# A two-layer convolution kernel: the first image's row differences on GpSimd, and the next image's group-mean product handed to TensorE two steps later

## The chip, the cores and the metric

The kernel runs on one core of a Trainium2 chip. The metric is the time on the device, in microseconds (us), from start to end of one launch; a launch does the whole batch of eight images and both layers. Time before: 1755.58 us, the median of three runs (1754.55 to 1759.55). The profile below is of one execution, whose span from first to last instruction is 1756.5 us.

## The reference, cut to what matters

All data are fp32. The input `x` has 8 images of 128 channels by 64 x 64 pixels. Two layers are each added to their input:

```python
x = x + L0(_gn(x))   # deformable 3x3 convolution, batch norm, relu
x = x + L1(_gn(x))   # mixture of 3x3 convolutions
```

`_gn` normalises each group of four channels over an image by its mean and variance. The change lies in the second layer:

```python
pooled = jnp.mean(x, axis=(2, 3))
scores = jax.nn.sigmoid(pooled @ gate_w.T + gate_b)
_, indices = jax.lax.top_k(scores + gate_bias, 2)       # two of four experts
weights = scores at indices, divided by their sum        # w_dense: (8, 4), zero elsewhere
ye  = conv2d(x, w_e) + b_e for each of the four experts
out = sum_e(ye * w_dense[e]) + conv2d(x, shared_w) + shared_b
```

A convolution is linear in its weights, so for one image the chosen experts and the shared kernel can be mixed into a single 3 x 3 kernel before anything is convolved. That is what the kernel does.

## The kernel before, in words

**Stages.** `dense()` is the first layer and takes the first 1372 us. `layer1()` is the second; it fills the rest. (A second pass through both follows only if the offsets of the deformable convolution leave a fixed reach; for this input it is skipped.)

**The second layer's arithmetic.** The 3 x 3 convolution is done two output rows at a time, with a Winograd-like transform in the vertical direction. From the normalised, padded image `pad2` each group `g` of 16 output rows (NG = 4 groups per image) gets three row differences and sums in a tile `v`, made by `transform(g, which, engine)`:

- `which` 1: odd rows plus even rows, 128 partitions x 528 elements (L1018)
- `which` 2: even rows minus odd rows, 528 elements (L1020)
- `which` 0: rows minus the rows two below, 1056 elements (L1022); it serves both outer products

The mixed weights are transformed in the same way into four sets: `wmix[:, 0]`, `u1`, `u2`, `wmix[:, 2]`. Each of the four products `j` of a group (order 1, 2, 0, 3) is then three matrix products, one for each horizontal tap `kx`, 128 x 128 weights by 512 columns. In the profile each such fp32 product is two TensorE instructions, so a product `j` is 6 instructions, a group 24, an image 96, eight images 768. `collect` empties the four PSUM results of a group: `j` = 1 on ScalarE (L1080, into `t`), the others on VectorE (L1084, L1088, L1090), and the output rows go out by DMA.

**The order is written by hand.** The stage is under a manual schedule: each engine gets its instructions in the order in which the Python code emits them, and takes them in that order. Image `b`'s products are emitted by the last loop of `layer1()`. Everything that image `b + 1` needs ahead of its products is a generator, `prepare(b + 1)`, whose `yield`s cut it in steps. After each product `j` the loop takes two steps of it (three after `j` = 3), so 36 in an image; they are counted from 1 here. Before the change the steps are:

- steps 1 to 10: for eight chunks of 512 pixels, batch norm and relu of the first layer's result on ScalarE (L928), the residual addition on GpSimd (L930; for image 0 every second one is on VectorE), and two steps later the chunk's statistics on VectorE (L932)
- step 11: the statistics put together into `mv` on VectorE (L937)
- step 12: the product `pm` on TensorE that averages the means over a channel group (L940)
- step 13: the deviation `d` and `e` on VectorE; step 14: the product `pv` of the variances on TensorE (L950); steps 15 and 16: scale and shift (one GpSimd instruction at L111 among them)
- steps 17 to 20: the gate product `pg` (L972), scores, the choice of experts; the normalisation into `pad2` (L963, ScalarE) is strewn over these and the next steps
- steps 21 to 25: mixing of the weights on VectorE (L1039: four instructions, L1047, and L1050 to L1052 for `u2` and `u1`)
- steps 26 to 33: the twelve transforms; step 34: the results are handed over

**Image 0 has no image ahead of it to hide behind.** `prepare(0)` runs to its end before any product. It is cut more finely: the weights are mixed for one `kx` at a time (so L1039 takes 384 elements and not 1152, and L1050 to L1052 take 128), and the products of its first group go `kx` by `kx`, all four `j` in each, so that TensorE can begin when the weights of `kx` = 0 are there. In the kernel before, transforms (0, 1) and (0, 2) of image 0 are on GpSimd, (0, 0) is on VectorE after the weights of `kx` = 0 (L1054), and the nine of groups 1 to 3 are on VectorE after all the weights (L1056 to L1062). The additions of image 1 come next in GpSimd's order, its statistics next in VectorE's.

Image 1's chunks 0 and 1 are emitted after group 0's product `j` = 1, its chunks 2 and 3 after the collection of that product on ScalarE. So ScalarE reaches chunk 2 only when TensorE has finished `j` = 1 of group 0.

Of the kernel before, what the change touches and what calls it, by code (L numbers as in the profile page):

```python
# [57 lines left out]
def deform_moe_conv(  # L58
# [18 lines left out]
    nc = tc.nc  # L77
# [777 lines left out]
    def layer1():  # L855
# [6 lines left out]
        with ExitStack() as st:  # L862
# [4 lines left out]
            NG = 4  # L867
# [52 lines left out]
            def prepare(b, made):  # L920
# [14 lines left out]
                    yield  # L935
                mv = small.tile([P, 2], F32, name="mv")
                nc.vector.bn_aggr(mv, stats)  # L937
                yield
                pm = ps_s.tile([P, 4], F32, name="pm", tag="pss")
                nc.tensor.matmul(pm[:, 0:1], lhsT=gsel, rhs=mv[:, 0:1], start=True, stop=True)  # L940
                yield
# [20 lines left out]
                def normalise(c):  # L962
                    nc.scalar.activation(  # L963
                        pad2[:, 1 + 8 * c : 9 + 8 * c, 1 : W + 1],
                        x1[:, c * CH : (c + 1) * CH].rearrange("p (h w) -> p h w", w=W),
                        AF.Identity, bias=shift, scale=scale,
                    )
# [45 lines left out]
                def transform(g, which, engine):  # L1013
                    v, r = vs[g], 2 * TR * g
                    even = pad2[:, r + 2 : r + 2 * TR + 2 : 2]
                    odd = pad2[:, r + 1 : r + 2 * TR + 1 : 2]
                    if which == 1:
                        engine.tensor_tensor(v[:, 2 * TR : 3 * TR], odd, even, ALU.add)  # L1018
                    elif which == 2:
                        engine.tensor_tensor(v[:, 3 * TR :], even, odd, ALU.subtract)  # L1020
                    else:
                        engine.tensor_tensor(  # L1022
                            v[:, 0 : 2 * TR], pad2[:, r : r + 2 * TR],
                            pad2[:, r + 2 : r + 2 * TR + 2], ALU.subtract,
                        )
# [4 lines left out]
                if b == 0:  # L1030
                    for c in range(4, NCH):
                        normalise(c)
                    transform(0, 1, nc.gpsimd)
                    transform(0, 2, nc.gpsimd)

                for kx in range(3) if b == 0 else (slice(0, 3),):
                    part = wmix[:, :, kx]
                    for e in range(NE):
                        nc.vector.scalar_tensor_tensor(  # L1039
                            part, experts[:, e, :, kx], wd[:, e : e + 1],  # L1040
                            part if e else shared[:, :, kx], ALU.mult, ALU.add,
                        )
                        if b:
                            normalise(4 + e)
                            yield
                    if b or kx == 1:
                        nc.vector.scalar_tensor_tensor(  # L1047
                            wmix[:, 1, 1], ident, inv, wmix[:, 1, 1], ALU.mult, ALU.add
                        )
                    nc.vector.tensor_tensor(u2[:, kx], part[:, 0], part[:, 2], ALU.add)  # L1050
                    nc.vector.tensor_tensor(u1[:, kx], u2[:, kx], part[:, 1], ALU.add)  # L1051
                    nc.vector.tensor_tensor(u2[:, kx], u2[:, kx], part[:, 1], ALU.subtract)  # L1052
                    if kx == 0:
                        transform(0, 0, nc.vector)  # L1054
                    yield
                for g in range(NG):  # L1056
                    if b or g:
                        transform(g, 1, nc.vector)
                        transform(g, 2, nc.vector)
                        yield  # L1060
                        transform(g, 0, nc.vector)
                        yield  # L1062
                made[b] = vs, (wmix[:, 0], u1, u2, wmix[:, 2]), bmix

            made, todo = {}, []
            for _ in prepare(0, made):
                pass
            for b in range(B):
                load(b + 2)
                ahead_of = prepare(b + 1, made) if b + 1 < B else iter(())  # L1070
                vs, us, bmix = made.pop(b)
                for g in range(NG):
# [115 lines left out]
```

## Time and profile before

| what | value |
|---|---|
| time, median of three | 1755.58 us |
| TensorE busy over the span | 1643.6 us (94%) |
| VectorE busy | 1189.7 us (68%) |
| ScalarE busy | 944.4 us (54%) |
| GpSimd busy | 939.6 us (53%) |
| last instruction of the first layer's batch statistics (L636) | 1372.8 us |
| first product of the second layer (L1102) | 1397.61 us |
| last of the 36 product instructions ahead of image 1's `pm` starts, ends | about 1414.6, 1415.16 us |
| image 1's `pm` starts on TensorE | 1426.38 us |
| first product after image 1's `pv` | 1432.20 us |
| first product of image 1 | about 1455.8 us |

How to read it: the busy share is an average over two very different stages. The rows with a point in time (microseconds from the start of the span, taken from the timeline in order of time) are those for the change: they all lie in the 60 us in which the second layer starts. From image 1 on, an image takes 42.0 us (from 1455.8 to 1497.8 TensorE is busy for all of it).

### The profile page before, as it was taken

What the parts mean: (1) busy time and instruction counts of PE and PEld (TensorE: products, weight loads), DVE (VectorE), ACT (ScalarE), POOL (GpSimd) and SP (SyncE); (2) the same over time, 40 slices, a digit from 0 to 9 for tenths busy, and PEclk for the clock granted to TensorE, in tenths of its full rate; (3) what the DMA queues carried; (4) which work ended last, traced back from release to release, by engine and by line L of the source; (5) the groups of instructions that cost most, each with busy time, mean ns of one, the idle gap of its engine ahead of it and who ended that gap; (6) DMA issues with size and microseconds to landing.
All of it is one profiled execution on the core that took longest, in us unless ns stands there. A gap on an engine that the chain in (4) does not pass through costs nothing. (4 is left out here: it accounts for less than half of the span.)

```text
span 1756.5 us, 21264 instructions
## 1 busy us (share of the span) xinstructions
PE 1643.6 (94%) x6490; PEld 931.0 (53%) x6490; DVE 1189.7 (68%) x1910; ACT 944.4 (54%) x1970; POOL 939.6 (53%) x1516
## 2 busy tenths in 40 slices
PE   4399999999999999999999999999999479999998
PEld 2155565566566556655665666566666234444443
DVE  4464874687467648755874587477665688888882
ACT  1465765576476557655765676476665323333330
POOL 3375576558557746764675657557763322322210
PEclk9599999999999999999999999999999689999999
DMA  4643774585368438744863675376663603444311
GB/s 133 124 121 93 154 179 106 115 194 137 93 133 203 121 82 168 180 106 103 193 150 94 134 187 143 98 137 151 161 158 87 267 25 144 155 156 154 123 49 62
DMA packets 197598, 235.84 MB, mean 134 GB/s; under 512 B 133964, under 2 KB 148048, under 8 KB 197478
## 3 DMA queue, kind: packets, MB, share of 16 engines
q0 software_dynamic: 94976, 124.94, 32.4%
q1 hardware_dynamic: 100556, 109.04, 20.7%
q8 instruction: 57, 0.93, 0.2%
q10 hardware_dynamic: 1946, 0.41, 0.1%
q14 instruction: 63, 0.52, 0.1%
HBM read 183.00 MB, written 50.82 MB: 133 GB/s over the span
## 5 line engine op out<-in xcount | busy, mean ns | idle before, releaser
L495 DVE TENSOR_TENSOR s<-xwts,ywts 100x324 f32<-100x324 f32 x968 | 691.5, 759 | 186.4 <-PE pq L506 160.1
L506 PE MATMUL pq<-s,xt 100*128 100x324 f32 x1936 | 696.8, 441 | 12.4 <-DVE s L495 6.7
L512 ACT COPY samples<-pq 128x324 f32<-128x324 f32 x968 | 423.9, 443 | 463.8 <-PE pq L506 458.1
L521 PE MATMUL py<-samples,dw_sb 128*128 128x384 f32 (+1 forms) x1584 | 625.1, 476 | 2.2 <-ACT y L532 2.1
L441 POOL DMA_DIRECT2D xwts<-tabx x863 | 527.2, 621 | 96.9 <-DMA ywts<-taby 52.6
L425 POOL DMA_DIRECT2D ywts<-taby x528 | 302.4, 587 | 365.8 <-DVE s L495 309.4
L506 PEld LDWEIGHTS pq<-s,xt 100*128 100x128 f32 x1936 | 322.4, 190 | 185.9 <-issue 48.7
L521 PEld LDWEIGHTS py<-samples,dw_sb 128*128 128x128 f32 x1584 | 299.5, 189 | 138.5 <-ACT y L532 6.5
L478 PE MATMUL pt<-ident,picked 128*100 128x128 f32 x968 | 194.2, 275 | 41.8 <-ACT picked L465 33.7
L478 PEld LDWEIGHTS pt<-ident,picked 128*100 128x100 f32 x968 | 121.6, 128 | 181.7 <-issue 80.0
L535 DVE BATCH_NORM_STATS2 ystats<-y 128x6 f32<-128x384 f32 (+1 forms) x88 | 48.2, 547 | 218.5 <-ACT y L532 218.5
L1102 PE MATMUL pc<-v,u 128*128 128x512 f32 x384 | 172.8, 599 | 9.2 <-DVE u L1051 9.2
L1102 PE MATMUL pc<-v,wmix 128*128 128x512 f32 x384 | 176.4, 605 | 0.0
L485 ACT COPY xt<-pt 100x512 f32<-100x512 f32 (+1 forms) x264 | 147.5, 559 | 2.2 <-PE pt L478 2.2
L313 PE MATMUL pc<-pad,offw_sb 128*32 128x504 f32 (+1 forms) x1152 | 142.2, 601 | 1.9 <-ACT pad L278 1.9
L1102 PEld LDWEIGHTS pc<-v,u 128*128 128x128 f32 x384 | 72.4, 190 | 98.3 <-issue 85.1
L1080 ACT ACTIVATE t<-pc,bmix 128x512 f32<-128x512 f32 x32 | 22.0, 687 | 182.5 <-issue 94.3
L1102 PEld LDWEIGHTS pc<-v,wmix 128*128 128x128 f32 x384 | 72.3, 191 | 88.6 <-issue 84.9
L457 ACT COPY picked<-pad 128x900 f32<-128x900 f32 x88 | 91.7, 1042 | 9.0 <-DMA xwts<-tabx 9.0
L608 ACT COPY samples<-samples 128x1188 f32<-128x1188 f32 x80 | 95.9, 1198 | 0.0
L930 POOL TENSOR_TENSOR x<-x,xt 128x512 f32<-128x512 f32 x32 | 47.0, 1496 | 85.3 <-ACT x L928 85.3
L930 POOL TENSOR_TENSOR pad<-pad,pad 128x512 f32<-128x512 f32 x28 | 39.6, 1442 | 71.6 <-ACT pad L928 71.5
(137 smaller groups left out, 897.1 us busy)
## 6 DMA issues: line engine op xcount, KB each, us to landing
ywts<-taby POOLq DMA_DIRECT2D x528, 116.0 KB, 4.3
pad<-in_x_dram SPq DMA_DIRECT2D x48, 512.0 KB
xwts<-tabx POOLq DMA_DIRECT2D x173, 116.0 KB, 3.8
out_dram<-yo SPq DMA_DIRECT2D x32, 512.0 KB
xwts<-tabx POOLq DMA_DIRECT2D x172, 92.8 KB, 3.8
yd<-y SPq DMA_DIRECT2D x80, 192.0 KB
xwts<-tabx POOLq DMA_DIRECT2D x173, 69.6 KB, 3.6
pad<-yd SPq DMA_DIRECT2D x16, 512.0 KB
```

The costliest lines, as they stand in the source:

```text
L313: nc.tensor.matmul(pc[32 * j : 32 * j + 32].rearrange("p (h w) -> p h w", w=W)[:, :, lo:hi], lhsT=offw_sb[:, k, :], rhs=pad[:, r : r + 8, ...
L425: engine.dma_start(out=y_wts[g % 2][r * Q : (r + NR) * Q, r].rearrange("p b c -> p (b c)"), in_=bass.AP(tensor=y_table[b].tensor, offset=y ...
L441: engine.dma_start(out=x_wts[g % 3][q:QQ:Q, :, lo:hi].rearrange("p t a b c -> p t (a b c)"), in_=bass.AP(tensor=x_table[b].tensor, offset= ...
L457: nc.scalar.copy(picked[g % 2][:, 1 : NT1 - 1], bass.AP(tensor=one.tensor, offset=one.offset, ap=[list(one.ap[0]), [T, NT1 - 2], [W, Q], [ ...
L478: nc.tensor.transpose(pt[0:QQ, c], picked[g % 2][:, c0 + c].rearrange("p y x -> p (y x)"), ident,)
L485: nc.scalar.copy(xts[g][0:QQ, c0 : c0 + n], pt[0:QQ, 0:n])
L495: nc.vector.tensor_tensor(s[0:QQ], x_wts[g % 3][0:QQ, c].rearrange("p a k r -> p k r a"), y_wts[g % 2][0:QQ, :, :, T * c : T * c + T].rear ...
L506: nc.tensor.matmul(pq.rearrange("p k r a -> p (k r a)"), lhsT=xts[g][0:QQ, c], rhs=ss.pop(n)[0:QQ].rearrange("p k r a -> p (k r a)"), star ...
L512: nc.scalar.copy(samples[g % 2][:, :, 2 : T + 2, T * c : T * c + T], pq)
L521: nc.tensor.matmul(py[:, first:], lhsT=dw_sb[:, 3 * ky + kx], rhs=samples[g % 2][:, n, first + ky : T + ky, kx : kx + W], start=(i == 0), ...
L608: nc.scalar.copy(samples[g % 2][:, :, 0:2], samples[(g - 1) % 2][:, :, T : T + 2])
L1102: nc.tensor.matmul(pc, lhsT=us[j][:, kx], rhs=vs[g][:, rows, kx : kx + W], start=(kx == 0), stop=(kx == 2),)
```

## The change

It has two parts. First, all twelve transforms of image 0 are given to GpSimd, in the order 1, 2, 0 of each group, and are emitted ahead of the mixing of its weights; VectorE makes none of them any more. For the later images they stay where they were. Second, for image 1 alone, two empty steps are put between the statistics `mv` and the product `pm`: `pm` and everything after it in `prepare(1)` come two steps later, so that `pm` stands on TensorE behind product `j` = 0 of group 1, and no longer ahead of it. The aim is to free VectorE at the start of the layer and to give TensorE work to do while image 1's statistics are not there.

```diff
                 mv = small.tile([P, 2], F32, name="mv")
                 nc.vector.bn_aggr(mv, stats)
-                yield
+
+                for _ in range(3 if b == 1 else 1):
+                    yield
                 pm = ps_s.tile([P, 4], F32, name="pm", tag="pss")
                 nc.tensor.matmul(pm[:, 0:1], lhsT=gsel, rhs=mv[:, 0:1], start=True, stop=True)
...
                 if b == 0:
                     for c in range(4, NCH):
                         normalise(c)
-                    transform(0, 1, nc.gpsimd)
-                    transform(0, 2, nc.gpsimd)
+                    for g in range(NG):
+                        for which in (1, 2, 0):
+                            transform(g, which, nc.gpsimd)
...
                     nc.vector.tensor_tensor(u2[:, kx], u2[:, kx], part[:, 1], ALU.subtract)
-                    if kx == 0:
-                        transform(0, 0, nc.vector)
                     yield
-                for g in range(NG):
-                    if b or g:
-                        transform(g, 1, nc.vector)
-                        transform(g, 2, nc.vector)
-                        yield
-                        transform(g, 0, nc.vector)
-                        yield
+                for g in range(NG if b else 0):
+                    transform(g, 1, nc.vector)
+                    transform(g, 2, nc.vector)
+                    yield
+                    transform(g, 0, nc.vector)
+                    yield
                 made[b] = vs, (wmix[:, 0], u1, u2, wmix[:, 2]), bmix
```

## The prediction, made before the changed kernel was run

> **What bounds the kernel now.** I read the page's forty slices first (43.9 us each).
>
> ```profile
> PE   4399999999999999999999999999999479999998
> PEclk9599999999999999999999999999999689999999
> ```
>
> TensorE is full except in the first two slices and in slices 32 and 33 (1361 to 1449 us) and at the very end, where the granted clock sinks too. The change touches nothing earlier, and after it an image takes 42.0 us of unbroken TensorE work. So only those holes are at stake. The waits from 1310 us on name them:
>
> ```profile
> PE pm L940 <- DVE mv L937: 25.4, 2, 14.2
> PE pc L1102 <- DVE u L1051: 9.2, 1, 9.2
> ```
>
> (who waited for whom: total us, times, longest). Image 0's `pm` took 14.2 us, so image 1's took 25.4 - 14.2 = 11.2. The chain of waits shows what lay ahead of it (start us, us, what):
>
> ```profile
> 1409.22 1.70 DVE v L1020
> 1410.92 2.25 DVE v L1022
> 1413.17 1.69 DVE v L1018
> 1414.86 1.69 DVE v L1020
> 1416.55 2.23 DVE v L1022
> 1418.78 1.20 DVE stats L932 x2
> ...
> 1425.96 0.38 DVE mv L937
> 1426.38 0.59 PE pm L940 x2
> 1426.97 5.25 PE pc L1102 x6
> ```
>
> The reader is to see VectorE doing image 0's transforms until 1418.8, then image 1's statistics, then `mv`, with TensorE waiting from 1415.16 to 1426.38. The six product instructions after it take 5.25 us; six others later take 2.70 (a step of 0.43 warm, 0.86 cold), so the hole costs 11.2 + 2.6 = 13.8 us. The timeline shows what VectorE and GpSimd do to each other:
>
> ```profile
> 1389.65 1.10 POOL L1018 TENSOR_TENSOR v<-pad 128x528 f32<-128x528 f32 x1 [2.31 <-ACT pad L963]
> 1389.95 0.82 DVE L997 SCALAR_TENSOR_TENSOR wd<-rank,score 128x4 f32<-128x4 f32 x1
> ...
> 1394.52 2.84 POOL L930 TENSOR_TENSOR x<-x,xt 128x512 f32<-128x512 f32 x2 [2.71 <-ACT x L928]
> 1395.00 1.23 DVE L1050 TENSOR_TENSOR u<-wmix 128x128 f32<-128x128 f32 x1
> 1396.27 1.23 DVE L1051 TENSOR_TENSOR u<-u,wmix 128x128 f32<-128x128 f32 x1
> 1397.54 0.29 DVE L1052 TENSOR_TENSOR u<-u,wmix 128x128 f32<-128x128 f32 x1
> ```
>
> L997, four elements, takes 0.82 us beside a GpSimd transform, against 0.16 for a later image: it ends when the transform ends. L1050 and L1051 take 1.23 beside GpSimd's additions, against 0.29 for L1052 after them. In the chain above, each VectorE transform beside additions takes 1.07 us more than alone (1.69 against 0.62, 2.25 against 1.17). They take turns, one for one.
>
> [...]statistics and the PSUM collections beside additions keep their 0.67 us.[...] The trace: full clock until about 1418.4, 3.2 us after the last product, half until 1432.
>
> **The change part by part.**
>
> *Nine transforms leave VectorE at the end, and (0, 0) in the middle.* From 1406.11 to 1418.78 is 12.7 us off the chain to `mv`, and 1.17 off the chain to the second weights.
>
> *GpSimd gets ten more.* A 528-element transform steps at 1.06 to 1.10 (1389.65, 1390.71)[...]. The 1056-element one isn't in the trace on GpSimd. Low: twice 1.06 = 2.12[...]. I take 2.17. All twelve alone: 4 x (1.08 + 1.08 + 2.17) = 17.3 us, 1389.65 to 1407. ScalarE's normalisation (done 1393.7) stays ahead of them.
>
> *The price is taken from VectorE's weight mixing,* which now meets transforms all along. By turns, a VectorE share[...] (0.62 at 528, 1.17 at 1056): 0.47 for L1039 at 384, 0.20 for L1050 to L1052 at 128, 0.07 for tiny ones. The walk: GpSimd's (0,0) from 1391.80 to 1393.97, L1005 1394.04; (1,1) 1395.12, L1008 1395.2; then nine turns: (1,2) + first L1039 1396.75; (1,0) + L1039 1399.39; (2,1) + L1039 1400.94; (2,2) + L1039 1402.49; (2,0) + L1050 1404.86; (3,1) + L1051 1406.14; (3,2) + L1052 1407.42; (3,0) + L1039 for `kx` 1 1410.06. Two additions with L1039s end at 1413.14, then GpSimd waits for ScalarE. VectorE goes on alone at its steps of before (0.65, 0.26, 0.33): `u1` of `kx` 1 at 1414.8, of `kx` 2, another 3.5 us on, at 1418.3.
>
> *TensorE's start* follows L1051, now 1406.3 and not 1397.6, 8.7 us later. First `kx`, cold: 5.3, to 1411.6. It waits 3.3 for `u1`, from 1414.9 does eight instructions (3.44), from 1418.4 eight more, to 1421.84. Then eighteen, one `j` more than before, 18 x 0.43 = 7.74: 1429.6. Before, the same place was 1432.06 (`pv`, with `pm` inside).
>
> *When `mv` is there.* ScalarE's chunk 2 is queued behind the collection of `j` = 1, which waits for 1418.4 + 0.86. Collection 1419.5, chunk 2 1420.1, first addition 1421.0 (0.88 after, as at 1408.10 to 1408.98). Six additions, nothing contending: 7.91 (the six of the next image, from 1460.07): 1428.9. Last statistics and `mv` 1.15: 1430.05. So `pm` at about 1430.1 waits 0.5 us, and products go on at 1430.25, against 1432.20. `pv`, still ahead in the new order, costs 0.14. Sum: **-1.8 us**. A cold restart at 1414.9 adds 1.7 to 3.4[...]: 0 to +1.5. I weigh it one in four.
>
> *The two steps* move `pv` behind `j` = 3 and `pg` into group 2. Behind `pm` on TensorE are image 0's products, each 2.6 us ahead of the next of these, time enough for `d`, `e` (0.6) and the scale (1.2). The later end of image 1's preparation: `pg` at 1435.6 against 1434.9, mixing done near 1448.5, transform (0,1) and (0,2) 1450.3 after one more collection; image 1 starts at about 1454. Margin 3.5 us, so nothing. PSUM has seven buffers and the collections come earlier than before: nothing. Loads and output DMA hang on points that hardly move: nothing.
>
> So the gain of a 13.8 us hole is nearly all spent on a start 8.7 us later and the 3.3 us hole in the first group. From 1755.58, weighing -1.8 and the cold case: 1754.1.
>
> **The rivals.**
>
> *L1039 doesn't contend* (only L1050 to L1052 and the small ones do). For it: no L1039 row is seen slowed. Against: L997 is the same kind. Then four L1039s run to 1397.2, L1051 ends 1399.85, later ones 1405.9 and 1411.5; TensorE does its last `kx` from 1411.6 to 1415.0, eighteen more to 1422.8; `mv` 10.6 after 1412.7, at 1423.3. Products at 1423.5 against 1432.2, less 0.14: -8.5, **1747.1**. With no contention at all `pm` would be at 1418.9 and the gain 13; the rows above exclude it.
>
> *VectorE doesn't get in between transforms,* since they stand ready one behind another, so that mixing waits for all of GpSimd's work. For it: one row only (L997) shows it getting in there; against: the chain's strict turns. From 1393.97, nine transforms 13.0 and two additions 2.15: 1409.2. Then L1005 to L1008, four L1039 and two: TensorE at 1413.1, and with `kx` after `kx` 5.3 + 3.4 + 3.4 + 7.7: 1433; `mv` 10.6 after 1422.9, `pm` 1433.6. +1.7, with a longer cold start +3: **1758**, slower.
>
> **How the numbers follow.** Forecast 0.60, faster rival 0.22, slower rival 0.18. Two in three of the faster rival's cases are at or above 1747. The slower one ends past 1760 if[...] the clock goes cold twice (+3), or image 1's 3.5 us margin is used up. Range 1747 to 1760. The bound of 0.3% is 5.3 us: faster takes the faster rival and a little of the forecast, 0.25; slower half of its rival and a little, 0.13; same 0.62.
>
> **What would show it.** L1039 for image 0 near 1.5 to 2.6 us instead of 0.62, and L1050 to L1052 above 1.2: turns are right; L1039 still at 0.62: the faster rival. The first product near 1406; a second wait of about 3 us on `u`; `pm` with under 1 us of wait near 1430; L1022 on GpSimd at 2.2 alone, about 2.6 with a turn. Wrong if image 1's first product waits for `v` or `u`, or if `mv` comes more than 2 us after TensorE asks.

## The result and the profile after

| | time, median | against before in the same comparison |
|---|---|---|
| before | 1757.57 us | |
| after | 1765.26 us | ratio 1.0044, 95% interval 1.0026 to 1.0063 |
| after, a second comparison | 1762.16 us (before there: 1756.99) | ratio 1.0037, 1.0026 to 1.0048 |

The change makes the kernel slower by about 0.4%: 7.7 us in the first comparison, 5.2 in the second. The forecast was 1754.1 us in a range of 1747 to 1760; the measured time lies above it.

The slices of the profile after, of the same kind as those shown of before (TensorE's busy tenths and its granted clock; a slice is 44.1 us):

```profile
PE   4399999999999999999999999999999299999998
PEclk9599999999999999999999999999999699999999
```

The second hole is narrower (one poor slice, a 2, where there were a 4 and a 7), and yet the kernel is slower. TensorE's waits from 1360 us on say where the rest is (who waited for whom: total us, times, longest):

```profile
PE pc L1102 <- DMA pad<-in_x_dram: 17.4, 1, 17.4
PE pm L942 <- DVE mv L937: 17.3, 2, 14.2
PE pc L1102 <- DVE u L1054: 3.2, 1, 3.2
```

The 17.4 is the wait for the first product (it is put down to a DMA; in the second execution the same wait is put down to `u` at L1054). It was 9.2. The `pm` row still has two waits: image 0's 14.2, as before, and another of 17.3 - 14.2 = 3.1. The timeline shows that this one is no longer image 1's:

```profile
1410.33 3.43 PE L1102 MATMUL pc<-v,u 128*128 128x512 f32 x4 [17.42 <-DMA pad<-in_x_dram]
...
1418.73 2.43 PE L1102 MATMUL pc<-v,u 128*128 128x512 f32 x4 [3.25 <-DVE u L1054]
...
1432.57 2.76 PE L1102 MATMUL pc<-v,wmix 128*128 128x512 f32 x6
1435.16 0.36 PE L942 MATMUL pm<-mv,gsel 128*128 128x1 f32 x2
...
1459.20 5.31 PE L1102 MATMUL pc<-v,u 128*128 128x512 f32 x12
...
1469.54 5.31 PE L1102 MATMUL pc<-v,u 128*128 128x512 f32 x12
1478.00 0.47 PE L942 MATMUL pm<-mv,gsel 128*128 128x1 f32 x2 [3.15 <-DVE mv L937]
1478.34 4.43 PE L1102 MATMUL pc<-v,wmix 128*128 128x512 f32 x6
```

The reader is to see: the first product, the wait of 3.25 us for the second tap's weights, image 1's `pm` at 1435.16 right behind its six new predecessors, without a wait; image 1's first product at 1459.20; and then image 2's `pm` at 1478.00, which waits 3.15 us where before it waited for nothing, and whose six followers take 4.43 us, not 2.84, on a clock that has fallen (granted 0.50 from 1478.16 to 1481.57, 1.00 around it). In the profile of before the same place reads:

```profile
1471.27 0.28 PE L940 MATMUL pm<-mv,gsel 128*128 128x1 f32 x2
1471.41 2.84 PE L1102 MATMUL pc<-v,wmix 128*128 128x512 f32 x6
```

**The scale.** The first layer, untouched by the change, ends at different times from execution to execution (GpSimd's L872, an instruction at the start of the second layer, stood at 1373.89 in the profile of before and at 1378.45 in that of after). So all below is counted from the start of L872, and the second layer is cut in two: its start, from L872 to image 1's first product, and the rest, from there to the end.

| execution | start | rest | second layer |
|---|---|---|---|
| before, profile | 81.9 | 300.7 | 382.6 |
| before, three further executions | 79.9, 79.9, 77.1 | 300.7 each | 380.6, 380.6, 377.8 |
| after, profile | 80.8 | 305.8 | 386.5 |
| after, two further executions | 79.1, 80.8 | 305.8 each | 384.9, 386.6 |

Means: start 79.7 before and 80.2 after, rest 300.7 and 305.8. Together +5.6 us, inside the interval of the second comparison (0.26 to 0.48% of 1757 us: 4.6 to 8.4). The start gives nothing; the rest loses 5.1 us.

### The profile page after: what moved, and what is told of

It is laid out like the page before. It is cut to its first block, busy times and chain, and to the rows that moved or that the text cites. A ratio compares the mean times of both kernels' runs of the same rounds, so it can differ in the third digit from the quotient of the medians.

```text
span 1765.0 us, 21267 instructions
## 1 busy us (share of the span) xinstructions
PE 1644.1 (93%) x6490; PEld 930.9 (53%) x6490; DVE 1192.1 (68%) x1900; ACT 944.9 (54%) x1970; POOL 954.6 (54%) x1526
## 5 line engine op out<-in xcount | busy, mean ns | idle before, releaser
L1102 PE MATMUL pc<-v,u 128*128 128x512 f32 x384 | 173.2, 600 | 20.7 <-DMA pad<-in_x_dram 17.4
L930 POOL TENSOR_TENSOR x<-x,xt 128x512 f32<-128x512 f32 x32 | 43.7, 1397 | 80.8 <-ACT x L928 80.8
```

Of the source, the lines that this page charges most:

```text
L1102: nc.tensor.matmul(pc, lhsT=us[j][:, kx], rhs=vs[g][:, rows, kx : kx + W], start=(kx == 0), stop=(kx == 2),)
```

## The experiments

Theory A: VectorE and GpSimd take turns (one instruction of the one, then one of the other), so that the moved transforms delay the mixing about as much as they free later; and the loss is image 2's statistics. Rivals: the first layer is slower for good by how the program lies (B) or merely spreads (C); the empty steps help and something else loses.

**The changed kernel again.**

> The changed kernel, once more, to see how much of its 7.7 us lies in the first layer, whose instructions are the same. In the two profiles at hand the second layer took 382.6 us before (1373.9, where GpSimd takes up L872, to 1756.5) and about 386.5 us after; the first layer took 4.5 us longer in the profile of after. Theory A (the loss is in the second layer: image 2's statistics come 3.15 us after TensorE asks for them, with a cold clock behind it): second layer again 386 to 387 us, the first layer anywhere within the 5 us by which executions of before differ; time 3 to 5 us above before. Rival B (the first layer is slowed for good, by where the program lies): first layer again 4 us longer than in before, time 7 to 8 us above before.

Measured: ratio 1.0037; second layer 384.9 us, 1.1 under the expected span: the first tap's products ran on the half clock for longer (their eight instructions took 3.75 and 3.17 us and not 3.43 and 1.89), so the wait for the second tap was 1.68 us and not 3.25, and the second tap's first four instructions took 1.98 us and not 2.43. First layer end 1374.30: only 0.4 us above the profile of before. Image 2's wait: 3.15 again. B loses its main evidence.

**The empty steps for image 2 too.**

```diff
-                for _ in range(3 if b == 1 else 1):
+                for _ in range(3 if b in (1, 2) else 1):
```

> After, with the two empty steps for image 2 as well, so that TensorE does six more product instructions (2.6 us) before it asks for image 2's means. Theory A: the wait of 3.15 us shrinks to about 0.6 and the clock stays full, so 4.2 us less than after in the second layer: about 382.3 us, level with before or 1 us faster. Rival B: 1 us or less changes against after, since the time is lost in the first layer. A further rival (the wait only moves to image 3): image 3's pm waits 2 us or more and the gain is under 3 us.

Measured: ratio 1.0037 (1.0022 to 1.0051), second layer 385.7 us. Image 2's `pm` waits 0.55, as expected, but image 3's now waits 3.14. The clock, though, stays full behind that wait (the six followers take 2.84 us), so the rest is 304.9 and not 305.8:

```profile
1519.88 0.38 PE L942 MATMUL pm<-mv,gsel 128*128 128x1 f32 x2 [3.14 <-DVE mv L937]
1520.12 2.84 PE L1102 MATMUL pc<-v,wmix 128*128 128x512 f32 x6
```

The further rival named there holds: the loss moves on to the first image that is not shifted.

**Each half of the change alone.** Transforms on GpSimd, no empty steps:

```diff
-                for _ in range(3 if b == 1 else 1):
-                    yield
+                yield
```

> After without the two empty steps: only the transforms on GpSimd. Theory A: the mixing contends as in after and mv comes at the same time; TensorE asks for image 1's pm 2.6 us sooner and so waits about 2.6 us there, no cold clock; image 2's pm then waits 0.6 instead of 3.15 and keeps its clock. Second layer about 384.6 us: 2 us above before, 2 us below after. If the two empty steps were worth their 2.6 us by themselves, this would be 2.6 us slower than after.

Measured: ratio 1.0026 (1.0018 to 1.0034); start 83.5, rest 300.7, second layer 384.2 us. Image 1's `pm` waits 2.42 us and its followers take 4.33: unlike what was expected, the clock did fall. Image 2's `pm` doesn't wait at all.

The empty steps alone, transforms as in before:

```diff
                 nc.vector.bn_aggr(mv, stats)
-                yield
+                for _ in range(3 if b == 1 else 1):
+                    yield
```

> Before with the two empty steps for image 1, transforms as in before. Theory A: mv at the same time as in before (1426.0), TensorE's wait shorter by the six instructions, 8.6 us and not 11.2, the clock cold after it all the same; image 2's pm waits under 1 us. Second layer 1.5 to 2.6 us shorter than in before: about 380.5 us. Rival: the shift alone makes image 1's preparation so late that image 2 waits 3 us too, and nothing is gained.

Measured: ratio 1.0017 (1.0007 to 1.0027); start 79.2, rest 305.8, second layer 384.9 us. Its two `pm` on TensorE, image 1's and image 2's:

```profile
1426.28 0.58 PE L941 MATMUL pm<-mv,gsel 128*128 128x1 f32 x2 [8.76 <-DVE mv L937]
...
1471.73 0.38 PE L941 MATMUL pm<-mv,gsel 128*128 128x1 f32 x2 [3.14 <-DVE mv L937]
```

The first wait is shorter by the six instructions; the second is the 3.14 us of after, with no transform on GpSimd but before's two. So the rival was right here, and the two halves separate:

| | start | rest |
|---|---|---|
| before (mean of four) | 79.7 | 300.7 |
| empty steps alone | 79.2 | 305.8 |
| GpSimd alone | 83.5 | 300.7 |
| both (mean of three) | 80.2 | 305.8 |

The empty steps cost 5.1 us in the rest, whatever the transforms; the transforms on GpSimd cost 3.8 us in the start, which the empty steps hide. The two halves are one execution each, and before's four starts lie between 77.1 and 81.9: GpSimd's 83.5 is above them all, but its 3.8 is rough. Set beside the one execution of before whose `mv` of image 1 came at the same time (52.4 us after L872 in both), the empty steps did gain what they were meant to gain at image 1, 2.7 us (79.2 and not 81.9), and lost 5.1 at image 2.

**The empty steps for every image.**

```diff
-                yield
+                for _ in range(3 if b else 1):
+                    yield
```

> Before with the two empty steps for all images from 1 on. Theory A (what comes after the empty steps is tied to TensorE's place, so the lag is set by the difference in steps between one image and the next): image 1 waits 8.7 us as with the shift of image 1 alone; images 2 to 7 each wait about 0.55, none 3.15, and the clock stays full; second layer about 383.3 us. Rival (a backlog from image 0's start that VectorE works off in its slack of 5.6 us an image): image 2 waits 0.55, images 3 to 7 nothing; about 380.5 us.

Measured: ratio 1.0014 (1.0000 to 1.0028), second layer 384.7 us. Images 3 and 4 on TensorE:

```profile
1514.89 0.38 PE L941 MATMUL pm<-mv,gsel 128*128 128x1 f32 x2 [0.56 <-DVE mv L937]
...
1557.74 0.38 PE L941 MATMUL pm<-mv,gsel 128*128 128x1 f32 x2 [0.55 <-DVE mv L937]
```

Every image from 2 to 7 waits 0.55 to 0.57, none 3.15, and none works it off: the lag is tied to TensorE's place, not to a backlog of VectorE's. An image now takes 1557.74 - 1514.89 = 42.85 us and not 42.03, so the wait costs 0.8 each, which the sum in the expectation had as 0.55.

**Is it GpSimd's reading?** GpSimd writes zeros instead of transforming, so that image 0's results are not computed; the times are of one execution:

```diff
-                        for which in (1, 2, 0):
-                            transform(g, which, nc.gpsimd)
+                        for lo, hi in ((2, 3), (3, 4), (0, 2)):
+                            nc.gpsimd.memset(vs[g][:, lo * TR : hi * TR], 0.0)
```

> After, but GpSimd fills image 0's row differences with zeros (a write of the same size, no reading of SBUF) and doesn't compute them. Theory A (VectorE's mixing is slowed because both read SBUF[...]): image 0's four mixing instructions of a tap take 0.62 us each again and not 1.5 to 2.6, u steps 0.29, the first product comes 8 to 9 us sooner against GpSimd's start (L872) than in after, image 1's pm waits under 1 us; image 2's still waits 3.15. Second layer about 374 us. Rival (any GpSimd work of that length slows VectorE): the mixing stays at 1 us or more.

Measured: second layer 378.5 us. First the timeline of after (GpSimd's transforms, VectorE's mixing of image 0), then that of this kernel:

```profile
1400.83 2.72 POOL L1024 TENSOR_TENSOR v<-pad 128x1056 f32<-128x1056 f32 x1
1403.52 1.41 POOL L1020 TENSOR_TENSOR v<-pad 128x528 f32<-128x528 f32 x1
1404.89 1.41 POOL L1022 TENSOR_TENSOR v<-pad 128x528 f32<-128x528 f32 x1
1406.26 2.72 POOL L1024 TENSOR_TENSOR v<-pad 128x1056 f32<-128x1056 f32 x1
...
1394.51 0.82 DVE L999 SCALAR_TENSOR_TENSOR wd<-rank,score 128x4 f32<-128x4 f32 x1
...
1401.33 5.39 DVE L1042 SCALAR_TENSOR_TENSOR wmix<-ew_sb,wd,wmix 128x384 f32<-128x384 f32 x3
1406.75 2.38 DVE L1053 TENSOR_TENSOR u<-wmix 128x128 f32<-128x128 f32 x1
1409.16 1.07 DVE L1054 TENSOR_TENSOR u<-u,wmix 128x128 f32<-128x128 f32 x1
```

```profile
1384.24 7.57 POOL L1037 MEMSET v<- 128x528 f32 x12
...
1386.91 0.16 DVE L999 SCALAR_TENSOR_TENSOR wd<-rank,score 128x4 f32<-128x4 f32 x1
...
1387.50 4.34 DVE L1005 TENSOR_SCALAR wd<-wd,tot 128x4 f32<-128x4 f32 x1
...
1394.20 0.61 DVE L1042 SCALAR_TENSOR_TENSOR wmix<-ew_sb,wd,sw_sb 128x384 f32<-128x384 f32 x1
1394.84 1.93 DVE L1042 SCALAR_TENSOR_TENSOR wmix<-ew_sb,wd,wmix 128x384 f32<-128x384 f32 x3
1396.81 0.29 DVE L1053 TENSOR_TENSOR u<-wmix 128x128 f32<-128x128 f32 x1
```

In after, a mixing instruction takes 5.39 / 3 = 1.80 us, and the `u` step beside a 1056-element transform 2.38; beside nothing that reads, they take 0.61 to 0.64 and 0.29. Here the zeros were over at 1391.81, before the mixing began, so this doesn't show mixing beside writes; it shows the mixing at full speed once no transform is beside it. But L999 shows it for one instruction of the kind: like the mixing it is a `scalar_tensor_tensor` of two SBUF tensors, and it took 0.82 us beside a transform in after and 0.16 in the midst of the zeros. So such an instruction kept its 0.16 us beside GpSimd's zeros, which read nothing, and took 0.82 beside a transform, which reads. Image 1's `pm` follows its predecessors without a wait (start 71.4), image 2's waits 3.14 again (rest 307.2, with a longer half clock behind it: the six products take 5.47 us). The first product came at 26.8 after L872, 5.1 sooner than in after, and not 8 to 9: L1005 stood for 4.34 us, until the last of the twelve zeros was written.

**Where the missing 3 us were.** The second layers with GpSimd's transforms were 1.6 to 3.9 us above before's 382.6, their times 4.4 to 7.7 above before's. A kernel with ten more instructions on GpSimd and no more work (`idle` is a new tile; the line that makes it is left out):

```diff
                     transform(0, 2, nc.gpsimd)
+                    for i in range(10):
+                        nc.gpsimd.memset(idle[:, i : i + 1], 0.0)
```

> Before with ten writes of one column (128 x 1) on GpSimd behind its two transforms of image 0, where GpSimd idles for 11 us: as many instructions more on GpSimd as the change has, and no other work. The kernels with all transforms on GpSimd measured 3 us more than their second layers explain. Theory B (the first layer is slowed by how the program lies): this kernel is 2 to 4 us slower than before too, its second layer unchanged at 382.6. Theory C (the excess is spread of the first layer over executions, or belongs to the moved work): within 1.5 us of before.

Measured: ratio 0.9997 (0.9983 to 1.0011). This speaks against B, which had 2 to 4 us. But its second layer was not unchanged: 378.4 us. So before was run with its profile three more times, and after once more:

> Before, once more, for its second layer's length (from GpSimd's L872 to the end), which so far is known from one execution: 382.6 us. The kernel with ten tiny writes took 378.4, because its first products ran cold for 1.1 us longer, image 1's additions on GpSimd came that much later, and VectorE's transforms of groups 1 to 3 met none of them: none of the five turns of 1.07 us. Theory D (before itself has both courses[...]; the 3 us of excess in the other kernels are not in their first layer, but before's 382.6 is its slow course): of the three looks at before at least one has a second layer of 377 to 380 us with uncontended transforms. Theory C (before is always 382.6, first layers spread): all three lie within 1 us of 382.6.

> As before_look_1, a second execution: theory D 377 to 383 us, with five, some or no contended transforms; theory C 382.6 within 1 us.

> As before_look_1, a third execution: theory D 377 to 383 us, with five, some or no contended transforms; theory C 382.6 within 1 us.

> After, a third execution, for the same purpose: its transforms are all on GpSimd ahead of the additions, so only the clock can vary: 384.5 to 387 us by both theories, with 3.15 us of wait at image 2's pm.

Measured: before 380.6, 380.6 and 377.8 us (theory D), after 386.6. VectorE's last transform of group 2 and the three of group 3 in the first of these executions of before, and those of group 3 in the third, with GpSimd's six additions beside them:

```profile
1410.56 2.33 DVE L1022 TENSOR_TENSOR v<-pad 128x1056 f32<-128x1056 f32 x1
1412.81 1.77 DVE L1018 TENSOR_TENSOR v<-pad 128x528 f32<-128x528 f32 x1
1414.51 1.77 DVE L1020 TENSOR_TENSOR v<-pad 128x528 f32<-128x528 f32 x1
1416.20 2.31 DVE L1022 TENSOR_TENSOR v<-pad 128x1056 f32<-128x1056 f32 x1
```

```profile
1404.74 10.80 POOL L930 TENSOR_TENSOR x<-x,xt 128x512 f32<-128x512 f32 x6 [12.51 <-ACT x L928]
...
1405.81 0.70 DVE L1018 TENSOR_TENSOR v<-pad 128x528 f32<-128x528 f32 x1
1406.42 0.70 DVE L1020 TENSOR_TENSOR v<-pad 128x528 f32<-128x528 f32 x1
1407.04 1.25 DVE L1022 TENSOR_TENSOR v<-pad 128x1056 f32<-128x1056 f32 x1
```

Four transforms took turns in the first, five in the profile that the prediction was read from, none in the third. There the additions did start among the transforms, but VectorE went on at full speed, and of GpSimd's 10.80 us the first addition took 4.68, until 1409.43, where the five after it took 1.26 each, 1.22 from one to the next; in the kernel with ten writes it was the same (4.38). What goes with this is when image 1's third addition starts: 35.1 us after L872 (five turns), 35.3 (four), 36.0 (none). That follows how long TensorE's first products ran on the half clock, which ended 27.4, 27.9 and 29.2 us after L872. Why a later start gave VectorE four instructions in a row, and not turns, stays open. Image 1's `pm` waited 11.2, 9.9 and 5.8 us accordingly.

**A version that beats both.** VectorE keeps the transforms but takes image 1's statistics first (`left[-1]` is image 0's `transform`, kept when its preparation ends; the two lines that keep it are left out):

```diff
                 nc.vector.tensor_tensor(gm, mv[:, 0:1], d, ALU.subtract)
+                if b == 1:
+                    for which in (1, 2, 0):
+                        left[-1](2, which, nc.vector)
...
                 nc.vector.reciprocal(inv, scale)
+                if b == 1:
+                    for which in (1, 2, 0):
+                        left[-1](3, which, nc.vector)
...
-                    if b or g:
+                    if b or g == 1:
                         transform(g, 1, nc.vector)
```

> Before, no transform moved to another engine and no empty steps: VectorE takes image 1's statistics ahead of the transforms of image 0's groups 2 and 3, which it does in the gaps of image 1's preparation (group 2 after d and e, group 3 after the shift). Theory A (what held image 1's mv was VectorE's order, not its load, and a step moved on TensorE comes back at the next image): mv ends at about 1418 on before's scale and not 1426.3, TensorE waits about 3 us and not 11.2, perhaps with a cold clock (1.5 us); image 2's pm waits nothing, as in before. Second layer 8 to 10.5 us shorter than before's 382.6. Rival (VectorE has no time left there either): the transforms push image 1's preparation back, image 1 or 2 waits 3 us or more, and under 5 us are gained.

Measured: 1748.63 us, ratio 0.9957 (0.9942 to 0.9972) against before; start 71.7, rest 300.7, second layer 372.4, 8.0 below the mean of before. Image 1's `pm` with its followers, then image 2's:

```profile
1419.14 0.38 PE L942 MATMUL pm<-mv,gsel 128*128 128x1 f32 x2 [2.43 <-DVE mv L939]
1419.38 4.53 PE L1112 MATMUL pc<-v,wmix 128*128 128x512 f32 x6
...
1462.96 0.28 PE L942 MATMUL pm<-mv,gsel 128*128 128x1 f32 x2
```

The wait falls to 2.43 us and nothing comes back at image 2: the moved transforms lie in VectorE's own pauses, and TensorE's order is not touched.

## Why the prediction was wrong, point by point

The third point below rests on these lines of VectorE, from image 1's mixing to image 2's `mv`, in the profile of before and then in that of after:

```profile
1438.36 1.41 DVE L1039 SCALAR_TENSOR_TENSOR wmix<-ew_sb,wd,sw_sb 128x1152 f32<-128x1152 f32 x1
...
1469.06 0.37 DVE L937 BATCH_NORM_AGGREGATE mv<-stats 128x2 f32<-128x48 f32 x1
```

```profile
1445.31 1.41 DVE L1042 SCALAR_TENSOR_TENSOR wmix<-ew_sb,wd,sw_sb 128x1152 f32<-128x1152 f32 x1
...
1467.48 2.32 DVE L1024 TENSOR_TENSOR v<-pad 128x1056 f32<-128x1056 f32 x1
...
1477.58 0.37 DVE L937 BATCH_NORM_AGGREGATE mv<-stats 128x2 f32<-128x48 f32 x1
```

- **Turns, one for one: right for the changed kernel.** Counted from L872, the first product was walked to 1406.3 - 1373.9 = 32.4; measured 31.9 in all three executions. The wait for the second tap was walked to 3.3; measured 3.25, 1.68 and 3.30, the short one where the first products had run cold for longer. After the two longer waits the clock fell for 3.41 us (granted 0.50 in the profile of after): the case that was weighed at one in four came in two of three executions. A 1056-element transform was put at 2.17 on GpSimd, an estimate of the author's near twice the 1.06 to 1.10 of 528 elements; the step was about 2.4 beside small VectorE work and 2.7 with a mixing instruction between. The walk's shares of VectorE, 0.47 at 384 elements, 0.20 at 128 and 0.07 for tiny ones, were estimates too, on the line through the measured 0.62 at 528 and 1.17 at 1056. Turns are no general rule, though: in the shortest execution of before VectorE took four in a row (1.25, 0.70, 0.70 and 1.25 us, as without GpSimd).
- **Image 1's `pm`: right.** Walked to 56.2, with 0.5 us of wait; measured 56.7, 55.1 and 56.8, with less than 0.1. Image 1's first product was put near 1454, so 80; measured 79.1 to 80.8.
- **"Margin 3.5 us, so nothing": the step that failed.** The margin was worked out to image 1's first product, and there it held: nothing waits at 1459.20. But VectorE has no pause from image 1's mixing to image 2's `mv`, and what had to be compared was image 2's `pm`. In before, `mv` ended at 1469.43 and TensorE asked at 1471.27: 1.84 us of slack. In after, image 1's mixing starts 13.9 us ahead of image 1's first product (1445.31 to 1459.20), in before 17.4 (1438.36 to 1455.78): 3.5 us lost to the steps. The stretch from there to the end of image 2's `mv` also grew, from 31.1 to 32.6 us, since the three transforms of group 3 now meet image 2's additions (2.65 us more; the 1056-element one takes 2.32 us, not 1.24), while two collections (1.2 us) now lie ahead of the mixing and no longer behind it. 3.5 + 1.5 - 1.84 = 3.2 of wait, 3.15 measured. The fallen clock, 3.41 us at half speed, costs 1.7 more; with 0.3 for a `pm` that no longer follows without a pause, 5.1. Of the forecast's two signs of being wrong, the first did not come, and the second, an `mv` more than 2 us late, came at image 2 and not at image 1.
- **The base: mis-sized.** The hole of 13.8 us, and -1.8 as its remainder, were read from one execution of before, the one with most turns. Against it the start gained 1.1 to 2.8 us, as walked; against the mean of the four executions of before it gained nothing (+0.5). So the term was off by 2.2 us, and image 2's wait by 5.1: together the difference from -1.8 to +5.6. Two slips beside these are small: by its own weights the forecast comes to about 1754.4 us and not 1754.1; and of the six additions read as "nothing contending" (7.91 us) the first had waited, 1.76 us against 1.27 for the others.
- **The rivals.** L1039 does contend, as the forecast had it from L997, an instruction of its kind: in after three mixing instructions took 5.39 us, and 1.93 with no transform beside them. VectorE does get in between transforms: each of the three had one transform ahead of it. The slower rival was right on the side alone: its cause isn't what happened.
- **Open.** The first layer of after ended at 1373.8 to 1378.5 in three executions, before's at 1368.8 to 1374.7 in four. Whether a microsecond of this is real was not settled; with ten more instructions on GpSimd the time did not rise, but the second layer there was itself 2.0 us under before's mean.

## What to carry to other kernels

When a step of one iteration is pushed back in an order that engines take strictly, follow the delay to the next place where anyone waits for that engine, which may be an iteration later; a margin at the nearest reader is not the slack of the loop. Work given to a second engine that contends with the first isn't free for being elsewhere: here three mixing instructions with a transform ahead of each took 5.39 us and not 1.93, 1.15 us more for each. Where two engines contend, read the base from several executions, since a fraction of a microsecond can go with another number of turns: here an addition that started 35.1, 35.3 and 36.0 us after L872 went with five, four and none.

## What the runs showed of the hardware that was not expected

- Who goes next when both engines have a queue. In after it was turns, one instruction each: three mixing instructions in 5.39 us, beside transforms of 2.72, 1.41 and 1.41 us. But in one execution of before VectorE took four transforms in a row while a GpSimd addition stood for 4.68 us; and in the kernel of the zeros a VectorE `tensor_scalar` of four elements (L1005, one SBUF tensor and a scalar), started among twelve back-to-back GpSimd writes, stood until the last of them was done: 4.34 us, to 1391.84, the last write ending at 1391.81; for a later image it took 0.23. So writes held this instruction, though they did not hold L999 (0.16 us).
- When the clock falls. In the clock records of before and after each stretch at a granted clock of 1.00 or 0.50 between two changes lasted a whole multiple of 3.41 us: the changes lie on a fixed grid. With that grid laid over TensorE's busy times in these two traces, from 100 us on each of the seven falls follows a piece of 3.41 us with 2.02 us or more of idle time, and none of the 939 other pieces at full clock has more than 1.51. So in these traces how a wait lies on the grid counts, beside its length. In after the wait of 3.25 us for the second tap had 2.02 us in one piece, and the clock fell. The waits of 2.42 and 2.43 us had about 2.0 and 2.4 us in one piece (the grid placed by where the products change speed), and six instructions after them took 4.33 and 4.53 us; image 3's wait of 3.14 us with the empty steps for two images was cut by the grid into 1.42 and 1.73, and the six after it took 2.84 us, the full clock's time.
